# Graph attention in layers 2 and 3: the last tile's twenty nodes stand twice, and one instruction makes the weights of both heads of a pair there

## The chip, the core and the metric

The kernel runs on one core of a Trainium2 chip. The core has a matrix engine (TensorE, PE in the profile; its loads of stationary data are PEld), a vector engine (VectorE, DVE), a scalar engine (ScalarE, ACT), GpSimd (POOL) and a synchronization engine (SP), each with an instruction queue of its own; ACT, POOL and SP also issue DMAs. Data lies in on-chip memory of 128 partitions (SBUF); matrix products are summed in PSUM. The metric is the device time of one execution in microseconds (us), as a median over runs.

## The reference

The program is a network of four graph layers over 2708 nodes with 512 features. Layers 0 and 1 average over neighbours; layer 2 is graph attention with eight heads of 64 features; layer 3 is graph attention with eight heads, an ELU, one more attention with a single head (called layer 4 here, although the reference has it inside its layer 3), and a two-layer MLP. After each layer come a residual and a normalization. The part that the change touches is the attention with eight heads:

```python
Wh = jnp.einsum('nf,hfo->hno', x, W)
src = jnp.einsum('hno,ho->hn', Wh, a[:, :O])
dst = jnp.einsum('hno,ho->hn', Wh, a[:, O:])
e = jax.nn.leaky_relu(src[:, :, None] + dst[:, None, :], ALPHA)
e = jnp.where(adj_mask[None, :, :], e, NEG)
attn = jax.nn.softmax(e, axis=-1)
return jnp.einsum('hnm,hmo->hno', attn, Wh)
```

Since leaky_relu(s + d) is max(s + d, 0.2 (s + d)), its exponential is a maximum of two products of a factor that depends on the target node and one that depends on the source node. The kernel works with these factors, so that no exponential over the 2708 x 2708 matrix is needed.

## The kernel before

**Tiles.** Nodes are cut into NT = 22 tiles of P = 128. The last one (number 21) has 2708 - 21 x 128 = 20 nodes. `maskT` is the transposed adjacency, with source nodes on partitions: for each source tile a row of all target nodes, one byte each, in SBUF throughout. For tile 21 only partitions 0 to 19 hold anything; the others are zero.

**Projection** (`project`, L561). For each layer the weights go to the tile `w`, which comes from `weight_tile()` (L143): a pool with one buffer under the tag "w", so that the next one to ask for it waits until the last use of the one before is over. Eight DMAs of 128 KB on ACT's queue fill it (L572) and POOL copies eight more columns into it (L573). Then, for each tile t: the input tile is turned (`xT`, L126), eight matmuls make `pm` (L611), DVE copies the source factors to `dcol` (L616) and clamps the target factors (L618), ACT takes exponentials, `ecol` (L620) and `ucol` (L621), and `vcol` (L631), DVE scales the projected features with `ecol` into `R2` (L625), and POOL makes `bcol` from `ucol` (L632). `keep_v` (L596, L597, L600) turns the target factors to a row and stores it in DRAM. At the end of each block of columns, DVE makes small operands for the softmax divisors (`ue`, `parts_m`, `parts_c`; L638 to L641 with the helper at L555 to L559).

**Attention** (`heads_attention`, L690). Target nodes form two blocks of 11 tiles (1408 and 1300 columns). A run is one pair of heads over one block: 2 x 4 = 8 runs in each of layers 2 and 3. In a run, `Weights.load` (L666) fetches the target factors of one head as a row that is repeated on all 128 partitions (`v_bc`, 704 KB, on SP's queue, three buffers). The loop over the 22 source tiles then does, for both heads of the pair:

- `weights` (L672), one DVE instruction over the whole block: e = max(v_bc, ucol of this head) x maskT, into one of five buffers;
- `above` (L680), one ACT instruction: c is a step function of e in 8 bits, used to find which branch of the maximum was taken, into one of eleven buffers. It is a sigmoid, so ACT changes its function table between this and the exponentials of the projection;
- L839: for each of three parts of the columns and each head, PE adds R2 (128 x 64) times e into the PSUM tile `po`: the two heads lie in its two halves of partitions.

Every four tiles PE adds the c's into the divisors (`divisors`, L749). In the first run of a layer, and again in the third, matmuls over maskT for the divisors of a block stand at tiles 12, 16 and 20 (`masks`, L732). When a run has ended, ACT copies po to `oT`; folding (L721), dividing (L771 to L776) and, in layer 2, turning to rows and storing (L782, L792, L796) are spread over the first tiles of the following run. `pe()` ties PE's instructions to the order in which the program writes them; on the other engines a scheduler orders the instructions, by priority and by what is ready when.

The next layer's projection (`project` of layer 3, with `summed` at L874 as its source: o, rows of layer 2's output, is read from DRAM, divided, added to x2 and normalized, with L118 on ACT) begins while the last run ends. Its weights (L572) are loaded as soon as "w" is free, which before the change is at the start of layer 2's attention.

Of the kernel before, what the change touches and what calls it, by code (L numbers as in the profile page):

```python
# [18 lines left out]
P = 128  # L19
D = 512  # L20
# [10 lines left out]
def kernel(  # L31
# [504 lines left out]
    for g in range(4):  # L536
        rows_m = ident[:, 32 * g:32 * g + 3 * H].rearrange("p (h i) -> p h i", i=3)
        rows_c = ident[:, 32 * g:32 * g + 12].rearrange("p (k q i) -> p k q i", k=2, q=2)
        nc.vector.tensor_reduce(pick_m[:, g], rows_m, AX.X, OP.add)
        nc.vector.tensor_reduce(pick_c[:, g], rows_c, AX.X, OP.add)  # L540
    ucol = late.tile([P, NT, H], F32, name="ucol")
    ecol = late.tile([P, NT, H], F32, name="ecol")
    for c in (ucol, ecol, vcol, bcol):
# [17 lines left out]
    def project(name, source, layer, v_dram, cuts, turned=None):  # L561
# [12 lines left out]
        with ExitStack() as ph:  # L574
            sm = ph.enter_context(tc.tile_pool(name=f"{name}_s", bufs=2))
            ps_tr = ph.enter_context(tc.tile_pool(name=f"{name}_ptr", bufs=2, space=PSUM))
            ps_mm = ph.enter_context(tc.tile_pool(name=f"{name}_pmm", bufs=2, space=PSUM))
            ps_v = ph.enter_context(tc.tile_pool(name=f"{name}_pv", bufs=2, space=PSUM))
            width = max(z - a for a, z in cuts) * P
            xs = early(1, NT, lambda t: source(sm, t, rows(t)))  # L580
            xTs = early(0, NT, lambda t: transposed(ahead, ps_tr, xs(t), rows(t), "xT"))
            if turned:

                cuts_ = [(t, t + 1) for t in range(3)] + [(t, min(t + 2, NT)) for t in range(3, NT, 2)]
                parts = early(2, len(cuts_), lambda i: ready[i] if i in ready else turned(sm, *cuts_[i]))
                xTs = lambda t: parts(t if t < 3 else (t - 3) // 2 + 3)[:, :, ((t - 3) % 2 if t > 2 else 0) * P:][:, :, :P]
            vrows, bs, scaled = {}, {}, {}

            def keep_v(t):
                n = rows(t)  # L590
                a, z = next(c for c in cuts if c[0] <= t < c[1])
                if t == a:
                    vrows[a] = sm.tile([heads, width], F32, name="vrow", bufs=1)
                vrow = vrows[a]
                ps = ps_v.tile([P, P], F32, name="ps_v")
                nc.tensor.transpose(ps[:heads, :n], bs[t][:n, :heads], ident[:n, :n])  # L596
                nc.scalar.activation(vrow[:, (t - a) * P:(t - a) * P + n], ps[:heads, :n], AF.Exp, scale=ALPHA - 1.0)  # L597
                if t == z - 1:
                    cols = slice(a * P, a * P + (z - 1 - a) * P + n)
                    nc.sync.dma_start(v_dram[:, cols], vrow[:, :cols.stop - cols.start])  # L600

            for t in range(NT):
                n = rows(t)

                xT = xTs(t)
                if t + 1 < NT:
                    xTs(t + 1)
                pm = [ps_mm.tile([P, D // 2 + H], F32, name=f"pm{a}") for a in range(2)]
                for k in range(KD):
# [12 lines left out]
                for a in range(2):  # L622
                    to, src = R2[:n, t, a * D // 2:(a + 1) * D // 2], pm[a][:n, :D // 2]
                    if heads > 1:
                        scaled[t] = nc.vector.tensor_mul(to.rearrange("p (h o) -> p h o", h=hh),  # L625
                                             src.rearrange("p (h o) -> p h o", h=hh),
                                             ecol[:n, t, a * hh:(a + 1) * hh, None].to_broadcast([n, hh, HO]))
                    else:
                        nc.scalar.activation(to, src, AF.Copy, scale=ecol[:n, t, 0:1])
                if heads > 1:  # L630
                    nc.scalar.activation(vcol[:n, t, :], b[:n, :], AF.Exp, scale=ALPHA - 1.0)  # L631
                    nc.gpsimd.tensor_scalar(bcol[:n, t, :], ucol[:n, t, :], -STEP * (1.0 + 2.0 ** -22), None,  # L632
                                            op0=OP.mult)
# [12 lines left out]
            dd = dcol[:, :, :heads]  # L646
            nc.vector.tensor_mul(sq.rearrange("p (t h) -> p t h", h=heads), dd, dd)
            nc.vector.tensor_scalar(sq, sq, RANGE * RANGE, None, op0=OP.is_le, op1=OP.add,
                                    accum_out=okc[:, layer:layer + 1])
            return scaled.get(NT - 2)  # L650

    class Weights:
# [16 lines left out]
        def weights(self, b, h, j, v):  # L669
            c0, w = self.blocks[b][0] * P, self.width(b)  # L670
            e = self.pool.tile([P, self.W], F32, name="e", bufs=5 if self.W > 512 else 4)
            nc.vector.scalar_tensor_tensor(e[:, :w], v[:, :w], ucol[:, j, h:h + 1], maskT[:, j, c0:c0 + w],  # L672
                                           op0=OP.max, op1=OP.mult)
            return e

        def above(self, b, h, j, e):

# [12 lines left out]
    def heads_attention(name, att, as_rows, scaled, meanwhile={}):  # L690
# [4 lines left out]
        with ExitStack() as ph:  # L695
# [47 lines left out]
                return [lambda i=i: products(8 * i, 8 * i + 8) for i in range(3)], fold, keep  # L743

            def divisors(b, p, pair):
                for j, hs, cs in pair:
                    for h, c in zip(hs, cs):
                        for g, c0, c1 in groups(b):
                            pe(nc.tensor.matmul(p[32 * g:32 * g + 12, :c1 - c0], parts_c[:, j, h, :], c[:, c0:c1],  # L749
                                                start=(j == 0 and h == hs[0]), stop=(j == NT - 1 and h == hs[1])))  # L750

            def finish(b, h0, p, pair, oT, last):

# [66 lines left out]

            products, fold, keep = masks(0, pd[1])
            todo = {12: products[:1], 16: products[1:2], 20: products[2:], NT: [fold], NT + 2: [keep]}
            for r, (b, h0) in enumerate(runs):
                w = att.width(b)
                parts = [(c, min(c + 4 * P, w)) for c in range(0, w, 4 * P)]
# [4 lines left out]
                if r + 1 == len(runs):  # L830
                    for j, steps in meanwhile.items():
                        todo[j] = todo.get(j, []) + steps
                for j in range(NT):
                    with tc.issue_after(scaled.ins) if r == 0 and j < 3 else nullcontext():
                        es = [att.weights(b, h, j, v) for h, v in zip(hs, vs)]
                    cs = [att.above(b, h, j, e) for h, e in zip(hs, es)]
                    for i, (c0, c1) in enumerate(parts):
                        for k, (h, e) in enumerate(zip(hs, es)):
                            pe(nc.tensor.matmul(po[i][HO * k:HO * k + HO, :c1 - c0], R2[:, j, h * HO:(h + 1) * HO],  # L839
                                                e[:, c0:c1], start=(j == 0), stop=(j == NT - 1)))  # L840
# [3 lines left out]
                    pair.append((j, hs, cs))  # L844
                    for step in todo.get(j, ()):
# [523 lines left out]
```

## Time and profile before

| what | value |
|---|---|
| median of three runs | 3024.32 us (3019.14, 3024.32, 3027.32) |
| profiled execution, and its span | 3025.69 us, 3023.9 us |
| granted TensorE clock | 0.993 |

The stages, from a table of windows over the whole span. PE, DVE and ACT are busy us within the stretch:

| stretch (us) | what runs | length | PE | DVE | ACT |
|---|---|---|---|---|---|
| 0 to 560 | mask, layer 0 | 560 | 522.25 | 382.68 | 242.72 |
| 560 to 885 | layer 1 | 325 | 325.00 | 86.52 | 79.69 |
| 885 to 977 | projection of layer 2 | 92 | 91.72 | 29.51 | 27.18 |
| 977 to 1544 | attention of layer 2 | 567 | 550.48 | 559.33 | 523.38 |
| 1544 to 1643 | projection of layer 3 | 99 | 91.98 | 66.79 | 40.69 |
| 1643 to 2210 | attention of layer 3 | 567 | 543.40 | 557.04 | 521.25 |
| 2210 to 3024 | layer 4 and the MLP | 814 | 783.68 | 341.62 | 98.12 |

How to read it: a busy share over the whole span mixes stages with different limits, so a change in the attention of layers 2 and 3 is judged in those two stretches. A window shows how full each engine is there; the chain of waits shows what the last work waited for, step by step, with "issue" for time in which the engine waited for nothing that the profile shows. TensorE's busy time counts matmuls that are pipelined, whose ends are modelled. In the groups of instructions the columns are: line, engine, operation, output and inputs with their shapes, count, then busy us and the mean ns of one, then the idle time of the engine just before them with what ended it.

### The profile page before, as it was taken

What the parts mean: (1) busy time and instruction counts of PE and PEld (TensorE: products, weight loads), DVE (VectorE), ACT (ScalarE), POOL (GpSimd) and SP (SyncE); (2) the same over time, 40 slices, a digit from 0 to 9 for tenths busy, and PEclk for the clock granted to TensorE, in tenths of its full rate; (3) what the DMA queues carried; (4) which work ended last, traced back from release to release, by engine and by line L of the source; (5) the groups of instructions that cost most, each with busy time, mean ns of one, the idle gap of its engine ahead of it and who ended that gap; (6) DMA issues with size and microseconds to landing.
All of it is one profiled execution on the core that took longest, in us unless ns stands there. A gap on an engine that the chain in (4) does not pass through costs nothing.

```text
span 3023.9 us, 36506 instructions
## 1 busy us (share of the span) xinstructions
PE 2908.5 (96%) x14456; PEld 1616.0 (53%) x14456; DVE 2023.5 (67%) x2417; ACT 1533.0 (51%) x1764; POOL 222.4 (7%) x354
## 2 busy tenths in 40 slices
PE   7999999999999999999998999999989999999997
PEld 4447766448887333444465433443365555555565
DVE  5976639413333999999977999999954535445342
ACT  3546533112223899999964999999951000000001
POOL 1110101101110000000022000000000000000001
PEclk9999999999999999999999999999999999999999
DMA  4542325322222100011034000010061000000000
GB/s 114 115 92 59 93 64 150 119 60 94 74 75 76 34 30 29 28 39 34 22 123 128 35 29 29 32 46 27 19 168 45 4 25 14 25 15 15 14 21 20
DMA packets 115063, 168.91 MB, mean 56 GB/s; under 512 B 40836, under 2 KB 65285, under 8 KB 114882
## 3 DMA queue, kind: packets, MB, share of 16 engines
q1 hardware_dynamic: 86210, 105.02, 11.9%
q0 software_dynamic: 18784, 57.79, 6.7%
q10 hardware_dynamic: 9888, 3.67, 0.5%
q8 instruction: 116, 1.90, 0.3%
q14 instruction: 65, 0.53, 0.1%
HBM read 136.46 MB, written 44.64 MB: 60 GB/s over the span
## 4 chain that ended last, share of the span: by engine, by line
PE 62%; DVE 15%; issue 14%; ACT 4%; DMA 3%; POOL 1%; SPq 0%; DVEq 0%; POOLq 0%; ACTq 0%
PE pn L999 13%; PE po L839 12%; DVE e L672 9%; PE acc L506 7%; PE pm L228 6%; PE pm L611 5%; PE pl L974 5%; PE pl L965 5%; PE acc L460 4%; ACT c L680 3%; PE pd L749 2%; PE ps_tr L124 1%; DVE maskT L485 1%; DMA rows<-o_dram 1%; DVE places L252 0%
## 5 line engine op out<-in xcount | busy, mean ns | idle before, releaser
L672 DVE SCALAR_TENSOR_TENSOR e<-v_bc,ucol,maskT 128x1300 f32<-128x1300 f32 (+3 forms) x836 | 1184.7, 1479 | 322.4 <-PE pn L999 314.1
L680 ACT ACTIVATE c<-e,bcol 128x1300 fp8e4<-128x1300 f32 (+1 forms) x704 | 990.4, 1423 | 76.4 <-DVE e L672 29.6
L839 PE MATMUL po<-e,R 128*64 128x512 f32 (+2 forms) x4224 | 925.2, 550 | 38.4 <-DVE e L672 28.2
L839 PEld LDWEIGHTS po<-e,R 128*64 128x64 f32 x4224 | 348.6, 137 | 582.1 <-issue 387.6
L999 PE MATMUL pn<-e,R 128*128 128x512 f32 (+1 forms) x1056 | 413.4, 542 | 0.0
L999 PEld LDWEIGHTS pn<-e,R 128*128 128x128 f32 x1056 | 191.2, 190 | 199.1 <-issue 196.0
L967 ACT ACTIVATE w<-pl,b 128x256 f32<-128x256 f32 (+1 forms) x88 | 40.9, 465 | 373.1 <-PE pl L965 373.1
L460 PE MATMUL acc<-yH,kT 128*128 128x512 f32 x484 | 197.3, 408 | 5.1 <-ACT kT L335 5.1
L228 PE MATMUL pm<-w,xT 128*128 128x512 f32 (+1 forms) x384 | 181.0, 616 | 21.9 <-DVE yL L223 18.5
L460 PE MATMUL acc<-yL,kT 128*128 128x512 f32 x484 | 189.4, 391 | 0.0
L506 PE MATMUL acc<-yH,mf 128*128 128x512 f32 x484 | 188.5, 389 | 0.0
L506 PE MATMUL acc<-yL,mf 128*128 128x512 f32 x484 | 188.4, 389 | 0.0
L113 POOL TENSOR_TENSOR ln_rs<-ln_rs,half 128x1 f32<-128x1 f32 x88 | 57.1, 649 | 1542.4 <-DVE ln_rs L112 1407.7
L611 PE MATMUL pm<-w,xT 128*128 128x264 f32 (+1 forms) x704 | 165.3, 388 | 4.0 <-DVE R L625 3.0
L228 PE MATMUL pm<-weight,xT 128*128 128x512 f32 (+1 forms) x352 | 160.2, 598 | 2.3 <-DVE u L317 1.5
L965 PE MATMUL pl<-lin 128*128 128x256 f32 (+1 forms) x704 | 154.8, 374 | 2.8 <-DVE lin L868 2.8
L974 PE MATMUL pl<-lin,w 128*128 128x512 f32 (+1 forms) x352 | 157.4, 592 | 0.0
L965 PEld LDWEIGHTS pl<-lin 128*128 128x128 f32 x704 | 130.4, 192 | 33.7 <-issue 15.8
L503 ACT CAST mf<-maskT 128x1024 fp32r<-128x1024 fp8e4 (+1 forms) x66 | 64.4, 977 | 157.9 <-PE acc L506 154.7
L222 ACT CAST yH<-pm 128x512 fp32r<-128x512 f32 (+1 forms) x44 | 25.7, 585 | 232.2 <-PE pm L228 232.2
L611 PEld LDWEIGHTS pm<-w,xT 128*128 128x128 f32 (+1 forms) x704 | 127.3, 186 | 29.6 <-ACT xT L126 5.6
L228 PEld LDWEIGHTS pm<-w,xT 128*128 128x128 f32 (+1 forms) x384 | 72.1, 192 | 122.1 <-issue 101.0
(208 smaller groups left out, 2689.8 us busy)
## 6 DMA issues: line engine op xcount, KB each, us to landing
rows<-x_dram SPq DMA_DIRECT2D x63, 256.0 KB, 2.7
v_bc<-v_dram SPq DMA_DIRECT2D x16, 704.0 KB, 4.1
x_dram<-u POOLq DMA_DIRECT2D x42, 256.0 KB, 2.4
v_bc<-v_dram SPq DMA_DIRECT2D x16, 650.0 KB, 4.1
m<-in_adj_dram POOLq DMA_DIRECT2D x13, 677.0 KB, 8.7
rows<-in_x_dram SPq DMA_DIRECT2D x21, 256.0 KB, 3.0
r_dram<-u POOLq DMA_DIRECT2D x21, 256.0 KB, 3.4
rows<-r_dram SPq DMA_DIRECT2D x21, 256.0 KB, 2.6
```

What stands on the lines that cost most here:

```text
L228: order(nc.tensor.matmul(pm[:n], xT[:, k, :n], w[:, k, :], start=(k == 0), stop=(k == KD - 1)))
L460: nc.tensor.matmul(pa[t], kT[:, (t - b[0]) * P:(t - b[0] + 1) * P], y[:, j, :], start=(j == 0 and y is yH), stop=(j == NT - 1 and y is yL))
L503: nc.scalar.copy(mf[:, :g1 - g0, :], maskT[:, g0:g1, t * P:(t + 1) * P])
L506: nc.tensor.matmul(pa, mf[:, j - g0, :], y[:, j, :], start=(j == 0 and y is yH), stop=(j == NT - 1 and y is yL))
L611: nc.tensor.matmul(pm[a][:n, :D // 2 + heads], xT[:, k, :n], w[:, k, a, :D // 2 + heads], start=(k == 0), stop=(k == KD - 1))
L672: nc.vector.scalar_tensor_tensor(e[:, :w], v[:, :w], ucol[:, j, h:h + 1], maskT[:, j, c0:c0 + w], op0=OP.max, op1=OP.mult)
L680: nc.scalar.activation(c[:, :w], e[:, :w], AF.Sigmoid, bias=bcol[:, j, h:h + 1], scale=STEP, saturate=False)
L749: pe(nc.tensor.matmul(p[32 * g:32 * g + 12, :c1 - c0], parts_c[:, j, h, :], c[:, c0:c1], start=(j == 0 and h == hs[0]), stop=(j == NT - 1 ...
L839: pe(nc.tensor.matmul(po[i][HO * k:HO * k + HO, :c1 - c0], R2[:, j, h * HO:(h + 1) * HO], e[:, c0:c1], start=(j == 0), stop=(j == NT - 1)))
L965: nc.tensor.matmul(pl[:, :w], self.lin1[:, k, f * P:(f + 1) * P], h[:, k, :w], start=(k == 0), stop=(k == KD - 1))
L974: nc.tensor.matmul(pl[:n], gT[:, f, (t - t0) * P:(t - t0) * P + n], self.lin2[:, f, :], start=(f == 0), stop=(f == KF - 1))
L999: nc.tensor.matmul(pn[k][:, :w], R2[:, j, k * P:(k + 1) * P], e[:, :w], start=(j == 0), stop=(j == NT - 1))
```

## The change

In layers 2 and 3 the last tile's twenty nodes are put on the partitions twice: on 0 to 19 for the first head of each pair, and on 32 to 51 for the second. Then one e and one c hold the weights of both heads of the pair at that tile, and both heads' matmuls read the same e, each with its own columns of R2. R2 is zero in the rows of the other head.

- maskT's rows 0 to 19 of that tile are copied to rows 32 to 51 by one DMA, once.
- At the last tile of the projection, POOL clears columns 20 to 31 of xT and copies its twenty columns to 32 to 51; the eight matmuls then give 52 rows. ecol, ucol and R2 are made in two rounds, for rows 0 to 19 with the even heads and rows 32 to 51 with the odd ones: two exponentials for ecol and four for ucol in place of one each, and four multiplications into R2 in place of two. bcol is made over 52 rows. Layer 4, with one head, clears rows 32 to 63 of R2 at that tile.
- `load_both` fetches, for a run, a tile with the row of the first head on partitions 0 to 31 and that of the second on 32 to 127, with two DMAs on SP's queue. The tile comes from `weight_tile()`, so it takes turns with the projection's weights in the one "w" buffer. That of the next run is asked for as soon as the run's e at the last tile is issued.
- The order of source tiles in a run becomes 0 to 9, 21, 10 to 20. Starts, ends and spread steps go by the position in this order.

```diff
+    LAST, TWIN, few = NT - 1, 32, rows(NT - 1)
+    assert few <= TWIN
+    nc.sync.dma_start(maskT[TWIN:TWIN + few, LAST, :N], maskT[:few, LAST, :N])
...
+                twice = heads > 1 and t == LAST
+                if twice:
+                    nc.gpsimd.memset(xT[:, :, n:TWIN], 0.0)
+                    nc.gpsimd.tensor_copy(xT[:, :, TWIN:TWIN + n], xT[:, :, :n])
+                elif t == LAST:
+                    nc.gpsimd.memset(R2[TWIN:2 * TWIN, LAST, :], 0.0)
+                m = TWIN + n if twice else n
...
-                        nc.tensor.matmul(pm[a][:n, :D // 2 + heads], xT[:, k, :n], w[:, k, a, :D // 2 + heads],
+                        nc.tensor.matmul(pm[a][:m, :D // 2 + heads], xT[:, k, :m], w[:, k, a, :D // 2 + heads],
...
-                nc.scalar.activation(ecol[:n, t, :heads], d, AF.Exp, scale=ALPHA)
-                nc.scalar.activation(ucol[:n, t, :heads], d, AF.Exp, scale=1.0 - ALPHA)
-                for a in range(2):
+                if twice:
+                    for k in range(2):
+                        at = slice(k * TWIN, k * TWIN + n)
+                        d2 = pm[1][at, D // 2 + k:D // 2 + heads:2]
+                        nc.scalar.activation(ecol[at, t, k::2], d2, AF.Exp, scale=ALPHA)
+                        for i in range(2):
+                            nc.scalar.activation(ucol[at, t, i::2], d2, AF.Exp, scale=1.0 - ALPHA)
+                        for a in range(2):
+                            view = lambda y: y.rearrange("p (h k o) -> p h k o", k=2, o=HO)[:, :, k]
+                            nc.vector.tensor_mul(view(R2[at, t, a * D // 2:(a + 1) * D // 2]), view(pm[a][at, :D // 2]),
+                                                 ecol[at, t, a * hh + k:(a + 1) * hh:2, None].to_broadcast([n, hh // 2, HO]))
+                else:
+                    nc.scalar.activation(ecol[:n, t, :heads], d, AF.Exp, scale=ALPHA)
+                    nc.scalar.activation(ucol[:n, t, :heads], d, AF.Exp, scale=1.0 - ALPHA)
+                for a in range(0 if twice else 2):
...
+        def load_both(self, b, h0):
+
+            c0, w = self.blocks[b][0] * P, self.width(b)
+            v = weight_tile().rearrange("p k a c -> p (k a c)")
+            for h, a, z in ((h0, 0, TWIN), (h0 + 1, TWIN, P)):
+                nc.sync.dma_start(v[a:z, :w], self.v_dram[h, c0:c0 + w].partition_broadcast(z - a))
+            return v
...
+            both = att.load_both(*runs[0])
+            order = [*range(10), LAST, *range(10, LAST)]
...
-                for j in range(NT):
-                    with tc.issue_after(scaled.ins) if r == 0 and j < 3 else nullcontext():
-                        es = [att.weights(b, h, j, v) for h, v in zip(hs, vs)]
-                    cs = [att.above(b, h, j, e) for h, e in zip(hs, es)]
+                for i_, j in enumerate(order):
+                    with tc.issue_after(scaled.ins) if r == 0 and i_ < 3 else nullcontext():
+                        if j == LAST:
+                            es = [att.weights(b, h0, j, both)] * 2
+                            cs = [att.above(b, h0, j, es[0])] * 2
+                            if r + 1 < len(runs):
+                                both = att.load_both(*runs[r + 1])
+                        else:
+                            es = [att.weights(b, h, j, v) for h, v in zip(hs, vs)]
+                            cs = [att.above(b, h, j, e) for h, e in zip(hs, es)]
```

More of the change, by code (lines that the diff above doesn't have):

```diff
@@ L631, in project @@
                     nc.scalar.activation(vcol[:n, t, :], b[:n, :], AF.Exp, scale=ALPHA - 1.0)
-                    nc.gpsimd.tensor_scalar(bcol[:n, t, :], ucol[:n, t, :], -STEP * (1.0 + 2.0 ** -22), None,
+                    nc.gpsimd.tensor_scalar(bcol[:m, t, :], ucol[:m, t, :], -STEP * (1.0 + 2.0 ** -22), None,
                                             op0=OP.mult)
@@ L745, in divisors @@
             def divisors(b, p, pair):
-                for j, hs, cs in pair:
+                for i, j, hs, cs in pair:
                     for h, c in zip(hs, cs):
@@ L749, in divisors @@
                             pe(nc.tensor.matmul(p[32 * g:32 * g + 12, :c1 - c0], parts_c[:, j, h, :], c[:, c0:c1],
-                                                start=(j == 0 and h == hs[0]), stop=(j == NT - 1 and h == hs[1])))
+                                                start=(i == 0 and h == hs[0]), stop=(i == NT - 1 and h == hs[1])))
             def finish(b, h0, p, pair, oT, last):
@@ L839, in heads_attention @@
                             pe(nc.tensor.matmul(po[i][HO * k:HO * k + HO, :c1 - c0], R2[:, j, h * HO:(h + 1) * HO],
-                                                e[:, c0:c1], start=(j == 0), stop=(j == NT - 1)))
+                                                e[:, c0:c1], start=(i_ == 0), stop=(i_ == NT - 1)))
                     if len(pair) == 4:
@@ L843, in heads_attention @@
                         pair = []
-                    pair.append((j, hs, cs))
-                    for step in todo.get(j, ()):
+                    pair.append((i_, j, hs, cs))
+                    for step in todo.get(i_, ()):
                         step()
```

## The prediction

> **What bounds the kernel now.** First the page.
>
> ```profile
> PE 2908.5 (96%) x14456; PEld 1616.0 (53%) x14456; DVE 2023.5 (67%) x2417; ACT 1533.0 (51%) x1764; POOL 222.4 (7%) x354
> PE   7999999999999999999998999999989999999997
> DVE  5976639413333999999977999999954535445342
> PE 62%; DVE 15%; issue 14%; ACT 4%; DMA 3%; POOL 1%; SPq 0%; DVEq 0%; POOLq 0%; ACTq 0%
> ```
>
> Read alone, the 96% says TensorE. But the change works in two stretches only, the attention of layers 2 and 3 (977 to 1544 and 1643 to 2210 us), where DVE's slices are full as well. So I asked for windows over four runs there (a run is one pair of heads over one block of target columns): two of layer 2's 1408-column block, the second with the mask products in it, and two of 1300 columns, one in each layer. The columns are PE, PEld, DVE, ACT and POOL busy, clock, DMA.
>
> ```profile
> 1075.76:1147.39 71.63, 69.72 (x460) 27.87 (x461) 70.79 (x50) 66.63 (x51) 0.00 (x0) 1.00 0.09 31
> 1218.85:1290.43 71.58, 70.75 (x553) 30.61 (x555) 69.84 (x51) 65.96 (x53) 0.00 (x0) 1.00 0.09 30
> 1381.41:1448.60 67.19, 65.79 (x459) 28.21 (x461) 67.05 (x53) 62.65 (x53) 0.00 (x0) 1.00 0.12 39
> 2006.80:2073.97 67.17, 64.80 (x450) 26.98 (x448) 67.17 (x53) 65.44 (x55) 0.56 (x2) 1.00 0.08 31
> ```
>
> DVE is idle for 0.0 to 1.7 us of a run. Both engines look full, so the chain of waits must say who waits for whom:
>
> ```profile
> 1759.16 3.29 DVE e L672 x2
> 1762.45 0.04 issue
> 1762.50 2.58 PE po L839 x9
> 1765.07 1.40 PE pd L749 x23
> 1766.47 5.00 PE po L839 x24
> 1771.47 0.03 issue
> 1771.50 0.02 DVEq L672
> 1771.52 0.41 issue
> 1771.92 3.29 DVE e L672 x2
> ```
>
> The pattern returns after 1771.92 - 1759.16 = 12.76 us, four source tiles. In the mask run, where TensorE is continuous, the same chain shows it doing four tiles of L839 in 10.12 us; with the 1.40 of L749 that is 11.5. So it waits some 1.25 us in four tiles. DVE sets the pace: eight weights in 12.76 us, 1.60 each. The groups by form say what one costs:
>
> ```profile
> L672 DVE SCALAR_TENSOR_TENSOR e<-v_bc,ucol,maskT 128x1408 f32<-128x1408 f32 x352 | 566.3, 1681 | 6.4 <-DMA v_bc<-v_dram 5.4 <-PE po L839 1.0
> L672 DVE SCALAR_TENSOR_TENSOR e<-v_bc,ucol,maskT 128x1300 f32<-128x1300 f32 x352 | 526.0, 1568 | 1.8 <-DMA v_bc<-v_dram 1.5
> L680 ACT ACTIVATE c<-e,bcol 128x1408 fp8e4<-128x1408 f32 x352 | 514.0, 1469 | 48.2 <-DVE e L672 20.2 <-PE pd L749 4.0 <-DMA w<-in_L_gnn_Wo_dram 0.3
> ```
>
> Neighbours overlap a little: ten in a row take 16.05 us at 996.10, so one adds (16.05 - 1.68)/9 = 1.60; nine of 1300 columns at 1524.36 take 13.44, so (13.44 - 1.57)/8 = 1.484.
>
> **What the skill says.** The Trainium skill, "Perfetto Trace Analysis", Identifying the Most-Contended Engine, calls busy time a poor measure for TensorE and a fair one for VectorE and ScalarE; the 1.25 us of waiting inside a 96% row agrees. "VectorE: DVE Perf Modes", Mode 1x, has one result per cycle and lane, at 0.96 GHz: 1408 columns are 1467 ns by estimate, against 1.60 us here. So the cost goes by columns, and 20 nodes cost what 128 do. "ScalarE: Activation LUTs", What ACT_TABLE_LOAD costs, has about 1283 ns for a change of table set and as much again for a drain; the trace has 1.28 us loads between Exp and Sigmoid at 979.34, 982.12 and 984.06, with no second gap of that size. I use 1.28.
>
> **The change, part by part.**
>
> *The merged weights.* Every run loses one e on DVE and one c on ACT (1.47 us, no bound here). TensorE keeps all its matmuls. Eight runs a layer: 4 x 1.60 + 4 x 1.484 = 12.3 us; two layers 24.7.
>
> *Mask runs.* In the run at 1218.85 TensorE is continuous from 1240.11 to 1273.67 and gives the pace (its own L749, L732 and L782 between). In the new order the last tile stands tenth, so TensorE comes to the mask stretch with less wait before it and the whole e isn't won. A tile is 10.12/4 = 2.53 us of TensorE; I give each of the four such runs 0.3 to 0.9 less, 0.4 as taken: -1.5. Elsewhere there is cover: the saved 1.6 a run against 1.25 a four-tile group, five groups a run.
>
> *Start of an attention.* At 977.59 e 1 and 2 run, then e 3 and 4, and DVE makes the last tile's R (984.67) and ue, splits and memsets up to 996; e 5 to 9 start at 987.22, 990.94, 992.65, 994.39 and 996.10. TensorE's first L839, at 985.61, waited 4.29 us for ue. Now R2 of the last tile comes in two rounds (rows 0 to 20, then rows 32 to 52), and the second exponential waits for the first round's multiplies. In the new ACT order a c with its Sigmoid table comes between, so two more table loads: load at 984.16, c to 986.92, load to 988.2, exponentials to about 988.4, R2 to 989.0. DVE's small work, about 4.6 us, comes behind it and e 6 starts at about 993.6, e 9 at 998.5 instead of 996.10: 2.4 us lost, 1.5 to 3.5, in each layer: -4.9. TensorE then starts near 989.5 instead of 985.6; ACT's 2.6 us are covered by its 5 us of idle time per run (71.63 - 66.63). The low end, 1.5, is if the e's slip in between the small operations; the high end, 3.5, if e 6 and e 8 must also wait for TensorE to give back their buffers, as there are five.
>
> *Layer 2 to 3.* The twin load takes the one "w" buffer, so layer 3's weights no longer come at 989 to 1020 but after the last run's tenth place, the last three of eight only about the final oT copies; the order puts them, the copies and dT ahead of the first tile's normalization (L118, 1540.25). First matmul 1544.63 becomes about +2.4, the third tile's rows (SP, 1544.20) about +4.8, of which the tiles' queue gives some back: -3, from -1 to -5. The eight loads themselves (128 KB, 2.2 us to land, 0.37 us of ACT's queue each, as at 992.66) leave the first run of layer 2 and come in the last: 3 us of ACT's queue moved from one run to another, both with about 5 us to spare. POOL's copy into w (0.74 us at 980.22) moves with them and stands ahead of the reciprocal roots (L113) of the first tile, waiting only for the last run's merged e: 0. Layer 4's weights fall inside its last run: 0.
>
> *Small pieces.* maskT's copy waits for ACT's last cast at 883.0 and stands on SP ahead of loads that are issued at 889.34: covered. Without that cover it would cost about 2.7 us, in which the page's loads of rows land. The twin loads of v: one pair more in each run, together as large as one v_bc (704 KB, 4.1 us to land by the page), issued on SP at the tenth place of the run before, some 70 us ahead of use and behind no v_bc load that still waits for a buffer; DMA share is at most 0.12 in the windows: 0. Late each time, it would cost up to 4.1 us a run. POOL's memset and xT copy end near 973.7 while TensorE is at the tile before until 976.42: 0; late they would cost about 1 us. The last tile's eight matmuls have 52 columns of stationary data in place of 20; loads of 20 columns take 2.55/12 = 0.21 us at 977.10 and those of 128 take 0.19 (L611's PEld, 127.3 us x704): 0. The multiplies that make R2 are four of half the width instead of two, 0.37 us each at most: they are in the 2.4 above.
>
> Sum: 24.7 - 1.5 - 4.9 - 3 = 15.3. The profiled execution took 3025.69 us (span 3023.9); less 15.3 is 3010.4. The median shown is 1.4 lower, so 3009; I say 3010.
>
> **Rivals.**
>
> *All of it is won.* The ends of an attention have cover: the small DVE work slips between e's while TensorE catches up, and project is TensorE-bound. 24.7 less mask loss 1.5 and 1 for the rest: 22, 3002. For it: TensorE runs half-paced from 985.6 to 989. Against: DVE has no gap there.
>
> *TensorE takes over.* If its real slack is the window's 0.8 to 1.9 us and the last tile's two heads, now arriving together, break the rhythm, half is won: 12.3 - 8 = 4, 3020. For: 96% busy. Against: 1.25 us of waiting per four tiles.
>
> *Slower: the shared buffer.* Place: layer 3's first projection. If w's eight loads aren't done when TensorE arrives (2.2 us each to landing, ACT's queue with waits between), serial landing is 8 x 2.2 = 18 us; with xT, rows and the norm behind ACT's queue doubling that, 36, and the 5 at the starts. From 20 us there the gain is gone; slower needs about 27. 24.7 - 1.5 - 4.9 - 30 = -12: 3036. For: the loads are late and on a busy engine's queue. Against: five of eight are issued within the run.
>
> *It doesn't do what it says* would be two e's kept at the last tile; the order shows one.
>
> **How the numbers follow.** My forecast 0.52, all won 0.20, TensorE 0.19, slower 0.09. 0.3% is 9 us, about what a measurement of this kernel tells from nothing: faster is below 3015.3. The forecast's ends: gain 24.7, mask 1.2 to 3.6, starts 3 to 7, layer 3 1 to 5: 9 to 19.5, so 3005 to 3015. All won lies at 3000 to 3005, TensorE at 3014 to 3023. The range from 3000 to 3020 leaves out slower and part of TensorE. Faster: 0.49 + 0.20 + 0.05 = 0.74; same: 0.03 + 0.14 = 0.17; slower 0.09.
>
> **What would show it.** L672 has 344 instead of 352 of each form. A run without masks lasts about 70.0 instead of 71.6 and 65.7 instead of 67.2, with DVE still idle at most 2 us; if DVE's idle time grows by 1.6, TensorE took over. Mask runs shorten by 1.0 to 1.3. Two more table loads near 988; e 9 2.4 us later after e 1 than 18.5. Project 3's first matmul some 2.4 us later after the last L749. If runs keep their length, or layer 3's start lies over 8 us later, I am wrong.

## The result, and the profile after

| what | before | after |
|---|---|---|
| median of ten runs each | 3024.32 us (3019.14 to 3030.77) | 3011.26 us (3007.16 to 3016.62) |
| ratio, with its 95% interval | | 0.9953 (0.9944 to 0.9961) |
| span of the profiled execution | 3023.9 us | 3005.7 us |

The change wins 0.47% of the time. The two profiled executions are 18.2 us apart, more than the medians, and not all of that is the change's: layer 2's first e starts at 977.59 us before and at 972.77 after, and in the experiments below at 973.3 to 978.5, so the stages ahead of it differ from one execution to the next by some 5 us. I therefore measure the change in the stretch that it touches, from layer 2's first e to the first of layer 3's last oT copies (oT is the copy that ACT makes of a run's result, three instructions at the end of each run). It took 1227.84 us before and takes 1215.50 after: 12.3 us less. What follows that stretch differs by 1.1 us.

Line numbers in the changed kernel: e is L697, c L713, po L880, pd's divisors L782, oT L890, the projection's matmuls L624. The groups by form of the profile after show the count that was forecast, 336 + 8 = 344 e of each width, the 8 with the twin rows as input being groups of their own:

```profile
L697 DVE SCALAR_TENSOR_TENSOR e<-v_bc,ucol,maskT 128x1408 f32<-128x1408 f32 x336 | 540.8, 1677 | 6.9 <-DMA v_bc<-v_dram 4.6 <-PE po L880 1.3 <-ACT oT L890 1.0
L697 DVE SCALAR_TENSOR_TENSOR e<-v_bc,ucol,maskT 128x1300 f32<-128x1300 f32 x336 | 502.6, 1562 | 2.3 <-PE po L880 1.4 <-DMA v_bc<-v_dram 0.9
L713 ACT ACTIVATE c<-e,bcol 128x1408 fp8e4<-128x1408 f32 x344 | 502.4, 1469 | 45.7 <-DVE e L697 17.8 <-PE pd L782 3.2
```

Windows over the same four kinds of run (plain and with masks in layer 2's first block, one of the second block in layer 2, one in layer 3), now cut at the first oT copy of a run; the columns are window, length, then PE, PEld, DVE, ACT and POOL busy, clock, DMA:

```profile
1122.51:1192.51 70.00, 68.44 (x459) 27.31 (x457) 69.19 (x48) 65.16 (x50) 0.00 (x0) 1.00 0.14 42
1192.51:1265.50 72.99, 71.50 (x549) 29.68 (x547) 69.64 (x49) 66.98 (x53) 0.00 (x0) 1.00 0.14 44
1330.12:1395.59 65.47, 64.36 (x459) 27.42 (x457) 65.47 (x51) 61.14 (x51) 0.00 (x0) 1.00 0.13 40
1990.85:2056.32 65.47, 63.58 (x448) 26.76 (x446) 65.47 (x52) 63.81 (x54) 0.55 (x1) 1.00 0.13 43
```

The plain run went from 71.63 to 70.00 us and the two of the second block from about 67.1 to 65.47. DVE is idle for 0.8 us or less in these three, as before: it still sets the pace. In the mask run it is idle for 72.99 - 69.64 = 3.4 us (2.1 before, by the same cut), while TensorE is for 1.5: there TensorE sets it for a part of the run. The chain of waits shows the same step of four tiles as before where DVE leads, with the 3.29 of two e and the 0.41 of issue ahead of them:

```profile
1758.61 4.99 PE po L880 x24
1763.60 0.03 issue
1763.63 0.02 DVEq L697
1763.65 0.41 issue
1764.06 3.29 DVE e L697 x2
1767.35 0.04 issue
1767.39 2.58 PE po L880 x9
```

From the starts of oT copies and of e in the traces, each kernel's stretch can be cut into parts. All are single profiled executions; the experiments are described below.

| part (us) | before | after | two_weights | exps_first | weights_on_sp | both_mended |
|---|---|---|---|---|---|---|
| layer 2, first run, from the first e | 79.58 | 80.92 | 82.51 | 78.32 | 80.91 | 78.34 |
| layer 2, other seven runs | 482.60 | 472.95 | 482.07 | 471.76 | 471.74 | 471.82 |
| last oT of layer 2 to first e of layer 3 | 103.14 | 110.07 | 107.48 | 108.79 | 103.82 | 103.19 |
| layer 3, first run | 79.56 | 79.56 | 81.15 | 78.32 | 79.52 | 78.32 |
| layer 3, other seven runs | 482.96 | 472.00 | 482.61 | 471.86 | 472.11 | 471.74 |
| sum | 1227.84 | 1215.50 | 1235.82 | 1209.05 | 1208.10 | 1203.41 |
| on the way from layer 2 to layer 3: TensorE idle | 7.15 | 10.74 | 9.44 | 8.33 | 8.06 | 7.48 |
| on that way: granted TensorE clock | 1.00 | 0.97 | 0.98 | 0.95 | 1.00 | 1.00 |

So the fourteen later runs win 9.65 + 10.96 = 20.6 us, the two first runs together lose 1.3 although each has an e less, and the way from layer 2 to layer 3 loses 6.9. Sums of single traces are good to about 1 us: two_steps (below), whose runs are as long as the changed kernel's, has 471.97 us for layer 2's other seven runs where the changed kernel has 472.95.

The last two rows of the table split the loss on the way. The windows over it, before and after, in the columns of above:

```profile
1539.77:1642.91 103.14, 95.99 (x491) 76.19 (x488) 68.51 (x229) 44.30 (x137) 32.28 (x64) 1.00 0.55 172
1526.64:1636.71 110.07, 99.33 (x491) 78.40 (x488) 68.82 (x228) 44.95 (x137) 31.70 (x66) 0.97 0.53 165
```

The same 491 records of TensorE fill 95.99 us before and 99.33 after. So 3.6 of the 6.9 us are waiting, and 3.3 are longer matmuls at a lower granted clock. The lower clock isn't a matter of this one execution alone: over the whole span the mean of the changed kernel's ten executions is 0.991, and that of 29 of the kernel before is 0.993.

### The profile page after: what moved, and what is told of

Same layout as the page of the kernel before. It is cut to its first block, busy times and chain, and to the rows that moved or that the text cites. A ratio compares the mean times of both kernels' runs of the same rounds, so it can differ in the third digit from the quotient of the medians.

```text
span 3005.7 us, 36523 instructions
## 1 busy us (share of the span) xinstructions
PE 2887.4 (96%) x14456; PEld 1609.2 (54%) x14456; DVE 2000.1 (67%) x2405; ACT 1516.9 (50%) x1760; POOL 225.0 (7%) x359
## 4 chain that ended last, share of the span: by engine, by line
PE 64%; DVE 21%; ACT 6%; issue 6%; DMA 3%; POOL 0%; DVEq 0%; SPq 0%; POOLq 0%; ACTq 0%
PE pn L1040 13%; PE po L880 12%; DVE e L697 12%; PE acc L506 7%; PE pm L228 6%; PE pm L624 6%; PE pl L1015 5%; PE pl L1006 5%; ACT c L713 4%; PE acc L460 4%; DVE places L252 2%; PE pd L782 2%; PE ps_tr L124 1%; DVE maskT L485 1%; DMA v_bc<-v_dram 1%
## 5 line engine op out<-in xcount | busy, mean ns | idle before, releaser
L697 DVE SCALAR_TENSOR_TENSOR e<-v_bc,ucol,maskT 128x1408 f32<-128x1408 f32 (+3 forms) x804 | 1133.7, 1467 | 323.9 <-PE pn L1040 314.7
L713 ACT ACTIVATE c<-e,bcol 128x1300 fp8e4<-128x1300 f32 (+1 forms) x688 | 967.7, 1423 | 73.7 <-DVE e L697 28.2
L880 PE MATMUL po<-e,R 128*64 128x512 f32 (+2 forms) x4224 | 907.2, 550 | 37.1 <-DVE e L697 22.0
L880 PEld LDWEIGHTS po<-e,R 128*64 128x64 f32 x4224 | 342.4, 137 | 568.9 <-issue 411.6
L228 PE MATMUL pm<-w,xT 128*128 128x512 f32 (+1 forms) x384 | 174.3, 597 | 23.0 <-DVE yL L223 18.5
L624 PE MATMUL pm<-w,xT 128*128 128x264 f32 (+1 forms) x704 | 168.5, 393 | 4.6 <-DVE R L650 3.1
L624 PEld LDWEIGHTS pm<-w,xT 128*128 128x128 f32 (+1 forms) x704 | 129.9, 190 | 30.2 <-ACT xT L126 5.0
L335 ACT ACTIVATE kT<-maskT 128x512 fp32r<-128x512 fp8e4 (+1 forms) x132 | 77.5, 594 | 118.1 <-PE acc L460 118.1
```

What stands on the lines that cost most here:

```text
L228: order(nc.tensor.matmul(pm[:n], xT[:, k, :n], w[:, k, :], start=(k == 0), stop=(k == KD - 1)))
L335: made = nc.scalar.activation(kT[:, :w], maskT[:, j, b[0] * P:b[0] * P + w], AF.Relu, scale=-1.0)
L624: nc.tensor.matmul(pm[a][:m, :D // 2 + heads], xT[:, k, :m], w[:, k, a, :D // 2 + heads], start=(k == 0), stop=(k == KD - 1))
L713: nc.scalar.activation(c[:, :w], e[:, :w], AF.Sigmoid, bias=bcol[:, j, h:h + 1], scale=STEP, saturate=False)
```

## The experiments

The theory: one e of DVE is what a run wins, and the rest of the 24.7 us is lost in two separate places, the exponentials at the start of an attention, and ACT's order at the start of layer 3's projection. The rivals: that TensorE, ACT's c or the new order of tiles made the gain; that the losses come from the small multiplications themselves, and from weights that are loaded too late.

**two_weights.** DVE makes the merged e twice, everything else of the change stays.

```diff
-                            es = [att.weights(b, h0, j, both)] * 2
+                            es = [att.weights(b, h0, j, both) for _ in range(2)]
```

> The changed kernel, but DVE makes the last tile's e twice, once for each head, into two buffers; the c is still shared. Theory (DVE's e sets the pace, one costs 1.60 or 1.48 us, and what the change lost of the 24.7 us lies at the starts of the attentions and at the start of layer 3's projection): all 24.7 us go and the losses stay, so the runs have the length they had before (71.6 and 67.1 us between the first copies of oT) and the time is some 11 us above before, about 3035. Rival (TensorE or ACT sets the pace and the gain came from the c or from the new order): runs stay at 70.0 and 65.5 us, time about 3011.

Measured: 3031.68 us, ratio to before 1.0029 (1.0021 to 1.0036). The windows over a plain run and one of the second block:

```profile
1129.84:1201.23 71.39, 69.48 (x459) 27.98 (x457) 70.78 (x49) 65.23 (x50) 0.00 (x0) 1.00 0.13 41
1338.00:1404.95 66.95, 65.78 (x458) 28.18 (x457) 66.95 (x52) 61.30 (x52) 0.00 (x0) 1.00 0.13 41
```

The run lengths of before are back, with the shared c and the new order in place. The gain is the e. The kernel is slower than before, because the costs of the change stay: in the table, its first runs are 2.93 and 1.59 us longer than those of before, with as many e, and the way to layer 3 is 4.3 longer. From this kernel to the changed one the sixteen runs win 1.59 + 9.12 + 1.59 + 10.61 = 22.9 us by the table. It came out 3 us below the 3035 that I had named, and its way to layer 3 is 2.6 us shorter than the changed kernel's for the same code. The traces show where: of the eight loads of weights one is issued behind the first of the last oT copies, not three as in the changed kernel, and the first tile's normalization comes 2.43 us behind that copy, not 5.24; half of the 2.6 us is less waiting of TensorE, half is shorter matmuls.

**two_steps.** ACT makes the c of the last tile twice, from the one e.

```diff
-                            cs = [att.above(b, h0, j, es[0])] * 2
+                            cs = [att.above(b, h0, j, e) for e in es]
```

> The changed kernel, but ACT makes the last tile's c twice, once for each head; the e is still shared. Theory (DVE's e sets the pace; ACT has some 4 us to spare in a run): runs stay at 70.0 and 65.5 us and the time within 2 us of the changed kernel's, 3009 to 3014. Rival (the c on ACT was part of the gain): runs are up to 1.4 us longer, the time up to 22 us more.

Measured: 3012.93 us, ratio 0.9959 (0.9946 to 0.9972), runs of 69.98 and 65.46 us. The saved c won nothing that these runs show: ACT isn't the bound.

**exps_first.** The six exponentials of the last tile are issued ahead of the four multiplications.

```diff
                         for i in range(2):
                             nc.scalar.activation(ucol[at, t, i::2], d2, AF.Exp, scale=1.0 - ALPHA)
+                    for k in range(2):
+                        at = slice(k * TWIN, k * TWIN + n)
                         for a in range(2):
```

> The changed kernel, but at the last tile of the projection all six exponentials stand ahead of the four multiplications into R2, so that ACT changes its table as often as before. Theory (the loss at the start of each attention is the wait of the second round's exponentials for the first round's multiplications, with two table loads): the fifth and later e come 1.5 to 2.8 us earlier after the first one, in both layers; 3 to 5 us less than the changed kernel, about 3007. Rival (the small multiplications and copies themselves cost it, or TensorE at half pace): under 1 us less.

Measured: 3007.78 us, ratio 0.9933 (0.9916 to 0.9949); its interval overlaps that of the changed kernel a little, so the trace has to decide. First the timeline of ACT and DVE at the start of layer 2's attention in the changed kernel (start, us, engine, line, operation):

```profile
979.20 1.28 ACT L713 ACT_TABLE_LOAD   x1
980.49 1.47 ACT L713 ACTIVATE c<-e,bcol 128x1408 fp8e4<-128x1408 f32 x1
981.98 1.28 ACT L637 ACT_TABLE_LOAD   x1
983.27 0.17 ACT L637 ACTIVATE ecol<-pm 20x4 f32<-20x4 f32 x1
983.47 0.48 DVE L642 TENSOR_TENSOR R<-pm,ecol 20x128 f32<-20x128 f32 x2 [1.47 <-ACT ecol L637]
983.57 1.28 ACT L713 ACT_TABLE_LOAD   x1
...
989.24 12.86 DVE L697 SCALAR_TENSOR_TENSOR e<-v_bc,ucol,maskT 128x1408 f32<-128x1408 f32 x8
```

Between two rounds of exponentials stands a c with its own table; DVE sits idle for 1.47 us until the second round is there, then does the whole of its small work, 983.99 to 989.24, ahead of e 6. In layer 3 DVE makes an e while the second round is on its way and is hardly idle, but there too the small work, 5.26 us, stands in one piece ahead of e 6. With the exponentials together (from the inserted line on, line numbers are two higher):

```profile
983.71 0.17 ACT L637 ACTIVATE ecol<-pm 20x4 f32<-20x4 f32 x1
984.44 1.28 ACT L715 ACT_TABLE_LOAD   x1
984.53 0.97 DVE L644 TENSOR_TENSOR R<-pm,ecol 20x128 f32<-20x128 f32 x4
987.42 1.67 DVE L699 SCALAR_TENSOR_TENSOR e<-v_bc,ucol,maskT 128x1408 f32<-128x1408 f32 x1
991.15 1.68 DVE L699 SCALAR_TENSOR_TENSOR e<-v_bc,ucol,maskT 128x1408 f32<-128x1408 f32 x1
```

e 6 is the last of these lines: 991.15 - 977.46 = 13.69 us after the first e, against 989.24 - 972.77 = 16.47 in the changed kernel and 990.94 - 977.59 = 13.35 before. The four multiplications without a wait take 0.97 us where the two of before took 0.73, so they aren't the cost. One thing that I had named didn't come: e 5 is 2.4 us later than in the changed kernel, not earlier. From e 6 on the e are earlier, e 9 by 2.4 us in layer 2 and by 1.1 in layer 3. By the table the first runs give back 2.60 and 1.24 us; 78.32 is 1.25 less than before.

**weights_on_sp.** The weights of layers 3 and 4 are loaded through SP's queue.

```diff
-                nc.scalar.dma_start(w[:, k, a, :D // 2].rearrange("p (h o) -> p h o", h=hh), src)
+                (nc.sync if layer else nc.scalar).dma_start(w[:, k, a, :D // 2].rearrange("p (h o) -> p h o", h=hh), src)
```

> The changed kernel, but the weights of layers 3 and 4 are loaded through SP's queue in place of ACT's; the buffer is still shared with the twin rows, so they are loaded as late. Theory (the loss of 6.9 us between the last oT copy of layer 2 and the first e of layer 3 comes from ACT's order: the load instructions stand in its queue and the first tile's normalization fell behind the copies): the first matmul of layer 3's projection comes 4.9 us after the first of the last oT copies as before, in place of 7.5, and the first e of layer 3 103 to 105 us after it in place of 110; 4 to 7 us less than the changed kernel, about 3006. Rival (the weights come too late, whatever the queue): first matmul stays at 7 us or more, no gain.

Measured: 3004.93 us, ratio 0.9932 (0.9918 to 0.9945), below the interval of the changed kernel up to an edge of 0.0001. The timeline of ACT at the end of layer 2's attention, first in the kernel before, where the first tile's normalization (L118) stands directly behind the first oT copy:

```profile
1539.77 0.58 ACT L849 COPY oT<-po 128x512 f32<-128x512 f32 x1 [0.49 <-PE po L839]
1540.25 0.81 ACT L118 ACTIVATE rows<-rows,ln_mv,ln_rs 128x512 f32<-128x512 f32 x1
```

then in the changed kernel:

```profile
1526.64 0.58 ACT L890 COPY oT<-po 128x512 f32<-128x512 f32 x1 [0.49 <-PE po L880]
1527.47 0.58 ACT L890 COPY oT<-po 128x512 f32<-128x512 f32 x1 [0.25 <-PE po L880]
1527.94 0.38 ACTq L577 DMA_DIRECT2D w<-in_L_gnn_W_dram  x1
1527.95 0.40 ACT L890 COPY oT<-po 128x276 f32<-128x276 f32 x1
1528.69 0.48 ACT L746 COPY dT<-pd 128x384 f32<-128x384 f32 x1 [0.35 <-PE pd L782]
1528.70 0.93 ACTq L577 DMA_DIRECT2D w<-in_L_gnn_W_dram  x2
1530.64 0.58 ACT L825 COPY e<-ps_t 128x512 f32<-128x512 f32 x1 [1.47 <-PE ps_t L815]
1531.40 0.58 ACT L825 COPY e<-ps_t 128x512 f32<-128x512 f32 x1 [0.17 <-PE ps_t L815]
1531.88 0.81 ACT L118 ACTIVATE rows<-rows,ln_mv,ln_rs 128x512 f32<-128x512 f32 x1
```

and with the loads on SP:

```profile
1527.39 0.58 ACT L890 COPY oT<-po 128x512 f32<-128x512 f32 x1 [0.49 <-PE po L880]
1527.87 0.81 ACT L118 ACTIVATE rows<-rows,ln_mv,ln_rs 128x512 f32<-128x512 f32 x1
1528.59 0.86 ACT L890 COPY oT<-po 128x512 f32<-128x512 f32 x2
1529.45 0.48 ACT L746 COPY dT<-pd 128x384 f32<-128x384 f32 x1
```

The first tile's normalization (L118) stands 0.48 us behind the first copy again, not 5.24 us; the first matmul comes at 4.86 us, not at 7.54. The loads also come earlier here: SP issues them from 1492.82 to 1497.80. That the order, and not the hour of the loads, held the matmul can be read in the changed kernel: its last load was issued by 1529.63, and the first matmul at 1534.18 followed the copy of the turned tile (1533.50, 0.58 long), which waits for L118. L118 itself waited for nothing but its place: what it needs from DVE was done at 1526.26 (L117, 1526.10 and 0.16 long), ahead of the first copy. The run last_tile_last below adds that late loads don't hold the matmul. Of the 6.25 us by which the way is shorter than in the changed kernel, 2.7 are less waiting of TensorE and 3.6 shorter matmuls (95.76 against 99.33 us), at a clock of 1.00.

**both_mended.** Both edits.

> The changed kernel with both edits: the six exponentials ahead of the multiplications, and the weights of layers 3 and 4 through SP's queue. Theory (the two losses are separate): the first attention runs take 78.3 us in both layers, 103 to 104 us lie between the last oT copy of layer 2 and the first e of layer 3; the span from layer 2's first e to layer 3's last oT copy is 1203 us (1215.5 less 5.2 and less 6.2); median 3001 to 3004. Rival (they overlap, one hides the other): no better than the better of the two alone, 3005 to 3008.

Measured: 3002.04 us, ratio 0.9921 (0.9908 to 0.9935); the stretch takes 1203.41 us, as named. Alone, the edits had shortened it by 6.45 and 7.40 us; together they do by 12.1. The parts that the edits are aimed at add up: the first runs are 3.8 us shorter here and in exps_first, the way 6.9 here and 6.25 in weights_on_sp. The 1.8 us that are missing are mostly the 1.2 by which layer 2's other runs happened to be longer in the trace of the changed kernel. So the two losses are separate. This kernel is faster than both the one before and the changed one.

**last_run_plain.** The six exponentials together, loads on ACT's queue, and the last run of each layer makes two e and c at the last tile, so that the buffer is free a run earlier.

```diff
-                        if j == LAST:
+                        if j == LAST and r + 1 < len(runs):
...
-                            if r + 1 < len(runs):
+                            if r + 2 < len(runs):
```

> The six exponentials ahead of the multiplications, and the last run of each layer makes two e and two c at the last tile from the ordinary rows, so that the shared buffer is free a run earlier and the weights come on ACT's queue long before the end. Theory (ACT's order at the end is what cost time, by the load instructions in it): first matmul of layer 3's projection at 4.9 us and its first e at 103 to 104 us, as with SP's queue; the last run of each layer is 1.5 us longer (67.0 and 67.9); 3004 to 3007. Rival (SP's queue helped for another reason): first matmul stays above 7 us, about 3009.

Measured: 3003.31 us, ratio 0.9922 (0.9907 to 0.9938). First matmul at 4.86 us, layer 3's first e at 102.37, last runs of 66.95 and 67.88 us; that e and the median come a little under the 103 to 104 and the 3004 to 3007 that I had named. SP's queue isn't needed: here the loads are on ACT's, all issued 50 to 100 us ahead of the last copies, and L118 stands 0.48 us behind the first copy again.

**last_tile_last.** Both edits, and the order of source tiles is 0 to 21.

```diff
-            order = [*range(10), LAST, *range(10, LAST)]
+            order = [*range(NT)]
```

> Both edits, and the order of the source tiles is 0 to 21 as before, so that the merged tile ends each run and the shared buffer comes free only at the end of a layer. Theory (the merged e saves the same wherever it stands; the place only decides when the weights can be loaded and how full TensorE is ahead of the mask products): runs of 70.0 and 65.5 us as with the tile tenth, the mask run of layer 2 (73.9 before, 72.7 with the tile tenth) within 1 us of 72.7, and the first matmul of layer 3 2 to 5 us later; 1 to 5 us more than with both edits alone. Rival (two heads' matmuls behind one e let TensorE run into a wait at the end of a run): runs longer by 1 us each, 16 us more.

Measured: 2999.55 us, ratio 0.9912 (0.9896 to 0.9927); the interval overlaps that of both_mended, and the stretch takes 1206.48 us, 3 more, as I had named. Its parts I had wrong. The runs of the second block take 64.27 us, 1.2 less than with the tile tenth; the first run of each layer takes 81.3 us, 3.0 more, which I didn't follow up; and the first matmul of layer 3 isn't 2 to 5 us later but 0.8 earlier. The groups by form say why the runs are shorter:

```profile
L699 DVE SCALAR_TENSOR_TENSOR e<-v_bc,ucol,maskT 128x1408 f32<-128x1408 f32 x336 | 540.9, 1675 | 3.7 <-PE po L882 3.7
L699 DVE SCALAR_TENSOR_TENSOR e<-v_bc,ucol,maskT 128x1300 f32<-128x1300 f32 x336 | 503.2, 1568 | 2.7 <-PE po L882 2.5
```

No e waits for v_bc any more (4.6 and 0.9 us in the changed kernel): the merged tile doesn't read v_bc, so with that tile last both rows are free an e earlier and the next run's second row comes in time. But in the second block that time wasn't idle. With the tile tenth, DVE does two steps of layer 3's first normalizations there in each run (1.29 us at 1331.23, 1396.70 and 1462.17 in both_mended); with the tile last they all come between 1517.31 and 1521.9, and layer 3's first e 4.5 us later (107.74). The steps' new place can be the reason for 1.6 of these 4.5 us at most, the longer waiting of TensorE (9.08 us against 7.48); the other 2.9 are longer matmuls, at a clock of 0.95 on the way against 1.00 in both_mended.

Here the eight loads are issued from 1517.42 to 1522.39, up to after the first oT copy at 1520.82, and the first matmul still comes 4.06 us behind that copy. So late weights alone don't hold it.

**last_but_in_last_run.** As last_tile_last, but the merged tile stands tenth in the last run of each layer.

> Both edits, with the merged tile last in a run as in the run before this, except in the last run of each layer, where it stands tenth so that the shared buffer is free for the next weights. Theory (with the merged tile last, both v_bc rows are read out one e earlier and the next run's second row no longer comes late; the time that this wins is partly what filled the wait, the first steps of the next layer's normalization, and those must be done later): runs of 69.1 and 64.3 us, no idle time of DVE for v_bc but in the last runs, first e of layer 3 103 to 106 us after layer 2's last oT copy, the stretch from layer 2's first e to layer 3's last oT copy 1196 to 1203 us against 1203.4 with the tile tenth everywhere; 2996 to 3002. Rival (the wait was free, since other work filled it): 1203 us or more, median 3001 to 3004.

Measured: 2999.29 us, ratio 0.9916 (0.9903 to 0.9930), which doesn't part it from both_mended; the stretch takes 1203.24 us against 1203.41. The rival holds as to the stretch. The median lies in the range that the theory named, but the stretch doesn't show a gain: five of layer 2's runs are 0.6 to 1.2 us shorter and its last 2.6, but the first run of each layer is 3.0 longer, and layer 3's first e comes at 107.55 us, with a clock of 1.00 on the way. L118 comes 3.75 us after the first copy and the first matmul at 7.72, although the loads were early and on SP:

```profile
1523.51 0.81 ACT L118 ACTIVATE rows<-rows,ln_mv,ln_rs 128x512 f32<-128x512 f32 x1 [1.22 <-DVE ln_mv L117]
```

Here it isn't ACT's order that holds it. ACT was idle for 1.22 us until DVE's last step of that normalization (L117, 1523.33) was done: the steps that had filled DVE's waits in the runs now start at 1517.72, behind the last e. So a late L118 can come from ACT's order, as in the changed kernel, or from DVE's.

## Why the prediction was right, and where a term was off

- **The bound.** DVE sets the pace of these runs, at 1.60 and 1.48 us for an e: shown by two_weights, which puts the e back and with it 1.4 us in the plain run and 1.5 in the one of the second block, while the c (two_steps) does nothing. That TensorE takes over, the second rival, is seen in mask runs alone.
- **The merged weights less the mask runs: 24.7 - 1.5.** Against two_weights the sixteen runs win 22.9 us; 23.2 were forecast. In the mask run of layer 2 and the run after it the two together went from 139.43 to 137.61 us, 1.8 where two e are 3.1; in layer 3, whose output isn't turned to rows by TensorE in those runs (138.62 to 135.68), the same pair won 2.9. So the mask loss is mostly layer 2's; that it comes from TensorE's turning to rows is argued from this, not shown.
- **The start of an attention: 4.9.** The first runs lost 2.93 and 1.59 us in two_weights against before, 4.5 in all, where 2.4 in each layer were forecast (twice that is 4.8). The cause is the one named, two rounds of exponentials with a c between them: exps_first takes back 3.8. The sizes by layer were not alike, as far as the traces show because DVE was idle for 1.47 us in layer 2 and hardly at all in layer 3. The granted clock in the first runs isn't what decides: in layer 3's it is 0.96 both in the changed kernel and in exps_first, and the run is 1.24 us shorter.
- **Layer 2 to 3: 3, and this term was mis-sized.** The beginning was right: the first matmul came 2.7 us later (2.4 forecast) and the third tile's rows 5.05 (4.8). That L118 falls behind the loads, the copies and dT was right too. Wrong was that "the tiles' queue gives some back". Measured from the first of the last oT copies, the normalizations of tiles 0, 3, 7, 12 and 21 start at 0.48, 11.69, 30.18, 50.74 and 95.07 us before, and at 5.24, 18.07, 36.61, 56.65 and 102.01 after: the delay of 4.8 us grows to 6 or 7 and stays. The loss is 6.9 us in place of 3, outside the 1 to 5 that were allowed for it. It is 3.6 us more waiting of TensorE and 3.3 of longer matmuls at a clock of 0.97 in place of 1.00; of the clock the sum had no term. What lowers the clock stays open. It is 1.00 on the way in the four kernels whose first matmul comes at 4.86 us and 0.95 to 0.98 in the four that load late on ACT's queue, but last_tile_last (first matmul at 4.06, clock 0.95) and last_but_in_last_run (7.72, clock 1.00) don't fit that.
- **Small pieces: 0.** No run shows one of them; with both places mended the stretch is 0.3 us from 1227.84 - 24.7, though this leaves no room for the 1.5 of the mask runs: within the 1 us or so to which single traces agree.
- **The sum.** -22.9 + 4.5 + 6.9 would be -11.5; the stretch shows -12.3, since two_weights' other runs are 0.9 us shorter than before's. 15.3 were forecast, the medians differ by 13.1. That 3010 came within 1.3 us of the 3011.26 measured is in part luck: the sum was 2 to 3 us too high, but 3024.32 - 15.3 is 3009.0 and was rounded up.

The rival of a slower kernel by way of the shared buffer had the place right: that is where most was lost. Its mechanism, loads in series that hold TensorE, didn't occur. (By its own terms the gain would have been gone from 18.3 us there, not from 20: 24.7 - 1.5 - 4.9.)

## What to carry to other kernels

Partitions that hold nothing of use aren't cheaper. Each e of the last tile runs over all 128 partitions for the sake of twenty, and where the program does leave partitions out, in the multiplications that make R2 (R in the profile), DVE takes about the same time. From the kernel before, for a full tile and for the last one:

```profile
976.92 0.76 DVE L625 TENSOR_TENSOR R<-pm,ecol 128x256 f32<-128x256 f32 x2 [0.34 <-ACT ecol L620]
984.67 0.73 DVE L625 TENSOR_TENSOR R<-pm,ecol 20x256 f32<-20x256 f32 x2
```

So on an engine that sets the pace, two instructions of which each needs a few partitions can be put on different partitions and made one; here that was worth 1.4 us on average in each of sixteen runs. Half of it was spent at the edges: when work is doubled in rounds, issue all of one engine's part of both rounds before the part that the other engine does with it, above all where that engine changes a table in between. And a DMA that is moved to a late place in the queue of a computing engine can change the order of that engine's work: look at what stands beside it, and give the load to an engine that does nothing else, or issue it long before. When a stage where TensorE is busy gets longer, compare the granted clock of that stage before looking for waits.

## What the runs showed that I had not expected

- A delay at the beginning of the projection isn't caught up: 4.8 us at its first tile were 6.9 at its end, over 22 tiles. TensorE is idle there for 7.15 of 103.14 us even before the change, and about half of the loss was a lower granted clock, not waiting.
- A wait for a late transfer can be in use: in layer 2's second block other work had been put there. Without the wait (last_tile_last) the runs became 1.2 us shorter, and that work came at the end of the layer. The stretch gained nothing, but this work isn't all of the reason: the first runs were 3.0 us longer in both layers, and a part of the 4.5 us on the way was the clock.
